# A reciprocals' row on GpSimd's queue, and two steps of the mask moved, in a masked attention kernel

## Chip, core and metric

The kernel runs on one core of one Trainium2 chip. The metric is the time of one execution in microseconds (us); the time before is the median of three runs. A profile, taken from one more execution, gives the span from the first to the last instruction and every instruction's place in it. Engines go by the profile's names: PE (TensorE), PEld (its weight load), DVE (VectorE), ACT (ScalarE), POOL (GpSimd), SP (SyncE, which here only issues DMAs). A "q" behind an engine's name is its queue of DMA issues and semaphores.

## What is computed

Eight batches of `x` (512 features by 1024 tokens, fp32) go through one attention layer with a 0/1 mask over tokens, and the result is added to `x`. Queries, keys and values are one and the same projection.

```
B, D, T = x.shape                       # 8, 512, 1024; NH = 8 heads, dk = 64
q  = transpose(x) @ Wq.T
qh = q split in heads
scores = einsum(qh, qh) / sqrt(dk)
logits = (scores * cmask + (1 - cmask) * -1e30) * rmask     # mask over keys, mask over queries
attn   = softmax(logits)
ctx    = attn @ qh
out    = x + transpose(ctx @ Wo.T)
```

A masked query has all its logits at zero, so its context is the mean over all tokens; masked keys get no weight in the other rows.

## The kernel before

Only the kept tokens are computed. For each batch the kept tokens (about half) are gathered into `NK` = 544 rows; the last row stands for the mean. All heads are taken in pairs: `pairs` holds 32 of them, numbered from 0, four to a batch (pair 11 is batch 2's last). A pair is worked through in `NC` = 5 slots, one for each chunk of 128 keys (the last is smaller). The tuple `(b, pr, c)` in `plan` names batch, pair in the batch, slot.

One slot does, in this order on all engines' queues: `scores` (TensorE, then ScalarE's exp into `e`, or `el` in slot 4), `open_slot`, the next pair's projection in slots 0 and 1, `weigh_behind` (the values weighed by earlier `e`), then the slot's tasks. Tasks come from a plan written out by hand: `put(b, pr, c, task, *args, rank=...)`. Within a slot, tasks of rank under 5 come in order of rank, then `contexts`, then those of rank 5 and over, then `issue_stores`. Every engine and every DMA queue runs its share strictly in the order in which it was written.

A gate orders TensorE against readers of its banks: `note(read)` keeps the first noted reader of a slot, and the first weighing matmul of the next slot waits for it; with none noted, it waits for the slot's own first exp:

```
gate[0] = reader[0] or reader[1]
```

What the change touches:

- `invert(pair)` runs in slot 0 of the next pair. It forms the reciprocals of the softmax sums (`ris`), turns them (`rt`), writes them in four small DMAs to a DRAM tile `row` (L788), and reads that back in two DMAs, spread over 64 partitions each, as `rb` (L793). SyncE issues all six. `contexts(pair)` multiplies by `rb`; for pair p it stands in slot 1 of pair p + 2, but for pair 27 in slot 3 of pair 28 and for pair 29 in slot 4 of pair 30. It begins with `sum_last` (L803).
- SyncE's queue also carries the pieces of `x` for batches ahead (L376), the rows stored to DRAM by `turn` (`xd`, L413), ranks (L450), output stores (L922) and `load_rows` (L902, L906), which loads tiles `g` to which results will be added.
- GpSimd's queue carries `gather` (L472, kept rows by index), stores of results to DRAM (`od`, L846) and `fetch` (L943), which adds rows of `od` to a tile `g` by index. A fetch needs its `g` loaded and its `od` stored. `finish_blocks` (VectorE, L913) then turns the tile for the store.
- Batch 0 is fetched by blocks: `place_blocks` (L891) copies the places of its tokens into `block_origin` in 16 small casts on VectorE, in slot 2 of pair 2.
- The mask is read a second time in another order (`mixed`). `rank_mixed` in pair 0, slot 3, turns it on TensorE, copies it on ScalarE (`mcol`, L1129), and ranks it by matmuls (L1133, L1134); the ranks go to DRAM and `load_ranks(1)` reads them back in slot 4. `search` (L462) uses them from pair 1, slot 2.

Of the kernel before, what the change touches and what calls it, by code (L numbers as in the profile page):

```python
# [305 lines left out]
def attention_of_kept_tokens(ctx, tc, x, mask, wq, wo, out, ident, wqT, woT, verdict, flag):  # L306


    nc = tc.nc
    B, D, T = x.shape  # L310
    P = 128
    DK = D // NH
    SCALE = 1.0 / math.sqrt(DK)
    ND = D // P
    NT = T // P
# [41 lines left out]
    seen = {}  # L357
# [3 lines left out]
    def bank(name, tag="t"):  # L361
        return ps.tile([P, NB], F32, tag=tag, name=name, bufs=2)
# [275 lines left out]
    def note(read):  # L638
        reader[0] = reader[0] or read.ins.name
# [139 lines left out]
    def invert(pair):  # L779

        b, pr = pair
        inverses(pair)
        ri = ris[pr % 2]
        rt = sb.tile([P, Q], F32, tag="rt", name=f"rt_{b}_{pr}")
        nc.vector.transpose(rt, ri)
        row = dr.tile([2, NC, A, Q], F32, tag="row", name=f"row_{b}_{pr}")
        for a in range(A):
            nc.sync.dma_start(  # L788
                row[:, :, a, :].rearrange("h c j -> (h c) j"), rt[a * Q : a * Q + 2 * NC, :]
            )  # L790
        rb = sb.tile([P, W], F32, tag="rb", name=f"rb_{b}_{pr}")
        for h in range(2):
            nc.sync.dma_start(  # L793
                rb[h * DK : (h + 1) * DK, :],
                row[h].rearrange("c a j -> (c a j)").partition_broadcast(DK),
            )
        rbs[pair] = rb
# [14 lines left out]
        nc.vector.tensor_copy(cT[:, NK - 1 : NK], qms.pop(pair))  # L812


    ods, gs, wholes, pos = {}, {}, {}, {}

    def place_outputs(b):
        if b not in ods:
# [68 lines left out]
    def place_blocks():  # L887

        for a in range(A):
            for j in range(A):  # L890
                nc.vector.tensor_copy(  # L891
                    block_origin[a * Q : (a + 1) * Q, j::A],
                    placed[j * Q : (j + 1) * Q, 0, a * (NT // A) : (a + 1) * (NT // A)],
                )
# [71 lines left out]
    def issue_stores(n=1):  # L966
        for store in stores[1]:
            store()
        stores[1] = stores[0][:n]
        stores[0] = stores[0][n:]  # L970

    pairs = [(b, pr) for b in range(B) for pr in range(ND)]
# [146 lines left out]
        for a in range(A):  # L1119
            nc.sync.dma_start(mixed[mids, a * Q : (a + 1) * Q], by_blocks[a])  # L1120

    def rank_mixed():


        BC = B * NT
        mixed, totals, spread, mcol = (seen[k] for k in ("mixed", "totals", "spread", "mcol"))
        pt = bank("mixed_t")
        nc.tensor.transpose(pt[:, :BC], mixed, ident[:BC, :BC])
        nc.scalar.copy(mcol, pt[:, :BC])  # L1129
        nc.vector.tensor_reduce(totals[:, 0:1], mixed, axis=AX.X, op=ALU.add)  # L1130
        nc.vector.tensor_copy(spread[:, 0, :], totals[:, 0:1].to_broadcast([BC, P]))
        pr = bank("rank_mixed_t")
        nc.tensor.matmul(pr[:BC, :P], mcol, seen["upto"], start=True, stop=False)  # L1133
        nc.tensor.matmul(  # L1134
            pr[:BC, :P],
            seen["before"].rearrange("p b c -> p (b c)"),
            spread[:, 0, :],
            start=False,
            stop=True,
        )  # L1140
        rank = seen["rank"] = keep.tile([BC, P], F32, tag="mixed_rank", name="mixed_rank")
        note(nc.scalar.copy(rank, pr[:BC, :P]))
        nc.sync.dma_start(ranks, rank)
# [35 lines left out]
    def plan():  # L1179
# [5 lines left out]
        def put(b, pr, c, task, *args, rank=0):  # L1185
            todo[b, pr, c].append((rank, task, args))
# [16 lines left out]
        for n in range(1, B):  # L1203
# [7 lines left out]
            else:  # L1211
                b = n - 2
# [69 lines left out]
            put(last, 3, 1 + i, begin_output, last, i, rank=7)  # L1282
        for d in range(ND):
            put(0, 3, 3 + d // 2, turn_outputs, d, rank=7)
        put(0, 0, 3, rank_mixed, rank=7)
        put(0, 0, 4, load_ranks, 1)
        put(0, 1, 1, place_all, rank=1)
        put(0, 1, 3, turn_places, rank=7)
        for b in range(2, B):
# [4 lines left out]
    def late(n):  # L1294
# [29 lines left out]
        for p, pair in enumerate(pairs):  # L1324
            b, pr = pair
            before = pairs[p - 1] if p else None
            final = p + 1 == len(pairs)
            for c in range(NC):
                scores(pair, c)
                open_slot()  # L1330
                if c == 0 and not final:
                    project(pairs[p + 1], 0)
                weigh_behind(pair, before, c)
                if c == 0 and before:
                    end_values(before)
                    if final:
                        inv = inverses(before)
                    else:
                        invert(before)
                tasks = sorted(todo[b, pr, c], key=lambda t: t[0])  # L1340
                for rank, task, args in tasks:
                    if rank < 5:
                        task(*args)
                if final and c == 0:
                    spread(before, inv)
                elif final and c == 1:
                    contexts(before)
                for earlier in settled[p, c]:
                    contexts(earlier)
                for rank, task, args in tasks:  # L1350
                    if rank >= 5:
                        task(*args)
                issue_stores(1 + (b == B - 1))
        last = pairs[-1]
        open_slot()
        weigh_behind(None, last, 0)
# [121 lines left out]
```

## Time and profile before

| | us |
|---|---|
| median of three runs | 677.13 (675.56 to 678.43) |
| the profiled execution's own time | 679.92 |
| its span | 677.9 |
| PE busy in the span | 621.4 (92%) |
| DVE busy | 362.0 (53%) |
| ACT busy | 360.5 (53%) |
| POOL busy | 184.1 (27%) |

The mean granted clock of TensorE was 0.963 of full speed. A busy share is an average over stages: the start (to about 41 us), 32 pairs of some 18 us, and the last batch's end (from about 645 us). Rows of a timeline give start, duration, engine, line, operation, and in brackets the idle time before and what ended it; a "x4" at the end means that four instructions were merged. Rows of the chain of waits give start, duration and what lay on the chain. A row of busy time by stage gives the stretch, its length, then the busy time of each engine with the number of its instructions.

### The profile page before, as it was taken

The page shows a single profiled execution, that of the slowest core. Times are in us where ns is not written, and L with a number is a line of the kernel's source. Part 1 is how long each engine was busy: PE and PEld are TensorE (multiplying, and loading weights), DVE is VectorE, ACT ScalarE, POOL GpSimd, SP SyncE. Part 2 cuts the span into 40 slices and gives each one's busy share as a digit, 9 for nine tenths or more (in the row PEclk, how much of TensorE's full clock was granted, in tenths as well). Part 3 has the DMA queues.
Part 4 walks back from the last instruction along what each step waited for, and adds up shares of the span by engine and source line. Part 5 has one row for each costly group of instructions (what it writes and reads, how often), then busy time and mean ns, then how long its engine had stood idle before and what let it go on. Part 6 is the DMA issues. An engine that isn't in the chain of part 4 may idle for free.

```text
span 677.9 us, 21834 instructions
## 1 busy us (share of the span) xinstructions
PE 621.4 (92%) x9056; PEld 413.2 (61%) x9056; DVE 362.0 (53%) x1113; ACT 360.5 (53%) x1010; POOL 184.1 (27%) x203
## 2 busy tenths in 40 slices
PE   6578989999999979999999999999999999998953
PEld 5345657677666656667666666676666655554422
DVE  6325885654564555555664566457645535234252
ACT  5127667656655645556656665656655445544300
POOL 4600221100134212341224304331334207006240
PEclk9688999999999989999999999999999999998985
DMA  8533663533366865696769777785857468744666
GB/s 277 170 122 98 197 192 89 165 97 113 103 197 141 215 185 154 205 252 164 198 227 247 169 187 247 195 196 150 233 135 144 130 212 154 211 146 78 128 197 190
DMA packets 98544, 117.10 MB, mean 173 GB/s; under 512 B 11785, under 2 KB 65625, under 8 KB 98426
## 3 DMA queue, kind: packets, MB, share of 16 engines
q1 hardware_dynamic: 77976, 75.71, 37.4%
q0 software_dynamic: 16224, 37.71, 24.4%
q10 hardware_dynamic: 4226, 2.10, 1.1%
q8 instruction: 75, 1.23, 0.8%
q14 instruction: 43, 0.35, 0.2%
HBM read 72.81 MB, written 42.67 MB: 170 GB/s over the span
## 4 chain that ended last, share of the span: by engine, by line
PE 76%; DMA 8%; DVE 7%; ACT 3%; SPq 2%; issue 2%; POOL 1%; DVEq 0%; ACTq 0%; POOLq 0%
PE s L662 17%; PE av L709 17%; PE pq L542 15%; PE po L834 15%; PE v L579 3%; DMA x<-in_x_dram 2%; PE pa L861 2%; PE xc L485 2%; DVE len L601 1%; ACT e L685 1%; DVE xc L488 1%; PE top L615 1%; PE s L676 1%; DMA rb<-row 1%; DMA g<-od,origin 1%
## 5 line engine op out<-in xcount | busy, mean ns | idle before, releaser
L685 ACT ACTIVATE e<-s,bias 128x544 f32<-128x544 f32 x256 | 180.3, 709 | 89.1 <-PE s L662 88.7
L709 PE MATMUL av<-e,v 64*64 64x272 f32 x2048 | 162.5, 398 | 7.9 <-ACT el L685 4.3
L662 PE MATMUL s<-qT 64*64 64x272 f32 x2048 | 155.8, 399 | 0.0
L542 PE MATMUL pq<-xc,wqT 64*64 64x272 f32 (+1 forms) x1984 | 127.5, 390 | 0.2 <-DVE xc L488 0.2
L709 PEld LDWEIGHTS av<-e,v 64*64 64x64 f32 x2048 | 85.5, 134 | 52.6 <-ACT cT L738 8.5
L834 PE MATMUL po<-woT,cT 128*128 128x256 f32 (+2 forms) x624 | 114.7, 363 | 0.0
L662 PEld LDWEIGHTS s<-qT 64*64 64x64 f32 x2048 | 82.3, 134 | 36.2 <-issue 6.9
L542 PEld LDWEIGHTS pq<-xc,wqT 64*64 64x64 f32 x1984 | 79.2, 134 | 37.5 <-issue 0.8
L943 POOL DMA_INDIRECT g<-od,origin x48 | 75.8, 1578 | 84.8 <-DMA g<-xd 60.5
L834 PEld LDWEIGHTS po<-woT,cT 128*128 128x128 f32 (+1 forms) x624 | 79.2, 164 | 28.8 <-issue 15.1
L846 POOL DMA_DIRECT2D od<-oc x56 | 31.3, 562 | 202.6 <-ACT oc L841 200.4
L472 POOL DMA_INDIRECT xin<-xd,source x40 | 39.8, 995 | 130.8 <-DMA row<-rt 71.8
L488 DVE COPY xc<-xc 128x512 f32<-128x512 f32 (+1 forms) x37 | 22.0, 613 | 61.4 <-PE xc L485 61.4
L559 DVE COPY qT<-pq 128x272 f32<-128x272 f32 x32 | 14.1, 439 | 70.2 <-PE pq L542 65.2
L841 ACT COPY oc<-po 128x256 f32<-128x256 f32 (+2 forms) x57 | 21.7, 382 | 55.8 <-PE po L834 55.8
L685 ACT ACTIVATION_READ_ACCUMULATOR e<-s,bias 128x1 f32 x256 | 50.2, 196 | 0.0
L588 DVE COPY v<-v 128x320 f32<-128x320 f32 x64 | 28.3, 483 | 34.3 <-PE v L579 34.3
L913 DVE STREAM_TRANSPOSE whole<-g 128x512 f32<-128x512 f32 x56 | 37.4, 687 | 13.8 <-DMA g<-od,origin 9.1
L601 DVE TENSOR_REDUCE len<-sq 128x10 f32<-128x640 f32 x32 | 26.1, 814 | 30.5 <-ACT sq L595 30.4
L738 ACT COPY cT<-av 128x272 f32<-128x272 f32 x62 | 21.1, 389 | 37.6 <-PE av L709 37.5
L425 ACT ACTIVATE junka<-x 128x512 f32<-128x512 f32 x64 | 40.2, 628 | 0.7
L462 DVE TENSOR_SCALAR_CACHE_REDUCE junk<-rank,key 128x1024 f32<-128x1024 f32 (+4 forms) x40 | 39.8, 996 | 0.0
(156 smaller groups left out, 633.4 us busy)
## 6 DMA issues: line engine op xcount, KB each, us to landing
xd<-xt SPq DMA_DIRECT2D x120, 128.0 KB
x<-in_x_dram SPq DMA_DIRECT2D x56, 256.0 KB
g<-xd SPq DMA_DIRECT2D x48, 256.0 KB
out_dram<-whole SPq DMA_DIRECT2D x20, 512.0 KB
rb<-row SPq DMA_DIRECT2D x60, 160.0 KB
od<-oc POOLq DMA_DIRECT2D x28, 256.0 KB
out_dram<-whole SPq DMA_DIRECT2D x16, 256.0 KB
rank<-ranks SPq DMA_DIRECT2D x7, 512.0 KB
```

The lines of the kernel that those rows point to most:

```text
L425: nc.scalar.activation(junk, xs[b][r][:, d, :], AF.Copy, accum_out=xbars[b][:, d, r : r + 1])
L462: nc.vector.tensor_scalar(junk[:, :n], rank[:, i * P :], key[:, col], 0.0, ALU.is_le, ALU.add, accum_out=found[:, col])
L472: nc.gpsimd.indirect_dma_start(out=xin[:n, :], out_offset=None, in_=rows_of_x[b], in_offset=bass.IndirectOffsetOnAxis(ap=searches[b][2][:n ...
L542: mm = nc.tensor.matmul(pqs[pair][hf][heads[h], :n], wqT[rows, d, at : at + DK], xcs[b][rows, d, hf * KH : hf * KH + n], start=(not cross ...
L601: nc.vector.tensor_reduce(lengths, sq.rearrange("p c (h d) -> p (c h) d", h=2), axis=AX.X, op=ALU.add,)
L662: nc.tensor.matmul(s[h][to, hf, :KH], qT[heads[h], at : at + DK], qT[heads[h], hf * KH : (hf + 1) * KH], start=True, stop=True,)
L685: act = nc.scalar.activation(e[:, h], of[h], AF.Exp, bias=biases[pair][:, c : c + 1], scale=SCALE, accum_out=acc[:, h, c : c + 1],)
L709: mm = nc.tensor.matmul(avs[pair][hf][heads[h], :KH], v[rows, c, heads[h]], e[rows, h, hf, :] if c < LAST else e[rows, h, :], start=(c == ...
L834: nc.tensor.matmul(po[j * n : (j + 1) * n, cols], cTs[b, pr][:, i * P : i * P + n], woT[:, pr, j * w + cols.start : j * w + cols.stop], st ...
L846: nc.gpsimd.dma_start(od[places[i], j * w : (j + 1) * w], oc[j * n : (j + 1) * n, :w])
L913: nc.vector.transpose(whole.rearrange("p (d a) n -> p a d n", a=A)[:, :, :, i * Q : (i + 1) * Q], gs.pop((b, i)).rearrange("p (a d f) -> p ...
L943: nc.gpsimd.indirect_dma_start(out=gs[b, i], out_offset=None, in_=ods[b], in_offset=bass.IndirectOffsetOnAxis(ap=origin[:, b, i : i + 1] i ...
```

## The change

Three things are moved.

1. The four stores of `row` are issued by GpSimd instead of SyncE. The two loads of `rb` leave `invert` for a function of their own, `load_inverses`, which runs at the end of slot 1 instead of in slot 0, behind that slot's `issue_stores`. For pair 27 (run in pair 28, the first of the last batch) it runs at the end of slot 0.
2. The 16 casts of `place_blocks` are made by GpSimd instead of VectorE.
3. `rank_mixed` is cut in two: `turn_mixed` (turning, copying, totals) stays in pair 0, slot 3; the ranking goes to slot 4 with rank 3, and `load_ranks(1)` to pair 1, slot 0.

```
 def invert(pair):
...
         for a in range(A):
-            nc.sync.dma_start(
+            nc.gpsimd.dma_start(
                 row[:, :, a, :].rearrange("h c j -> (h c) j"), rt[a * Q : a * Q + 2 * NC, :]
             )
+        inverted[pair] = row
+
+    def load_inverses(pair):
+
+        b, pr = pair
+        row = inverted.pop(pair)
         rb = sb.tile([P, W], F32, tag="rb", name=f"rb_{b}_{pr}")
         for h in range(2):
             nc.sync.dma_start(
...
 def place_blocks():
         for a in range(A):
             for j in range(A):
-                nc.vector.tensor_copy(
+                nc.gpsimd.tensor_copy(
                     block_origin[a * Q : (a + 1) * Q, j::A],
...
-    def rank_mixed():
-
+    def turn_mixed():
...
         nc.scalar.copy(mcol, pt[:, :BC])
         nc.vector.tensor_reduce(totals[:, 0:1], mixed, axis=AX.X, op=ALU.add)
         nc.vector.tensor_copy(spread[:, 0, :], totals[:, 0:1].to_broadcast([BC, P]))
+
+    def rank_mixed():
+
+        BC = B * NT
         pr = bank("rank_mixed_t")
-        nc.tensor.matmul(pr[:BC, :P], mcol, seen["upto"], start=True, stop=False)
+        nc.tensor.matmul(pr[:BC, :P], seen["mcol"], seen["upto"], start=True, stop=False)
...
-        put(0, 0, 3, rank_mixed, rank=7)
-        put(0, 0, 4, load_ranks, 1)
+        put(0, 0, 3, turn_mixed, rank=7)
+        put(0, 0, 4, rank_mixed, rank=3)
+        put(0, 1, 0, load_ranks, 1)
...
                 issue_stores(1 + (b == B - 1))
+                if before in inverted and (c == 1 or p == len(pairs) - ND):
+                    load_inverses(before)
```

More of the change, by code (lines that the diff above doesn't have):

```diff
@@ L812, in contexts @@
         nc.vector.tensor_copy(cT[:, NK - 1 : NK], qms.pop(pair))
-    ods, gs, wholes, pos = {}, {}, {}, {}
+    ods, gs, wholes, pos, inverted = {}, {}, {}, {}, {}
     def place_outputs(b):
@@ L1136, in rank_mixed @@
             seen["before"].rearrange("p b c -> p (b c)"),
-            spread[:, 0, :],
+            seen["spread"][:, 0, :],
             start=False,
```

## The prediction, made before the result was known

> **What bounds the kernel now.** I read the page first (its busy times, the first line), then busy time by stage (the other four: stretch, its length, busy time of TensorE, its weight load, VectorE, ScalarE and GpSimd with their instructions, TensorE's granted clock, the DMA engines' share, GB/s), then the order of time on each engine around the stages where TensorE is not full.
>
> ```profile
> PE 621.4 (92%) x9056; PEld 413.2 (61%) x9056; DVE 362.0 (53%) x1113; ACT 360.5 (53%) x1010; POOL 184.1 (27%) x203
> 41.50:61.40 19.90, 16.42 (x239) 10.20 (x238) 6.26 (x16) 11.96 (x36) 0.00 (x0) 0.85 0.12 31
> 76.30:95.00 18.70, 15.84 (x267) 10.12 (x263) 15.08 (x52) 11.33 (x32) 7.80 (x11) 1.00 0.77 234
> 236.00:262.20 26.20, 22.17 (x311) 14.62 (x313) 13.41 (x42) 12.49 (x37) 2.49 (x3) 0.87 0.69 189
> 262.20:334.74 72.54, 72.17 (x1124) 49.71 (x1127) 43.27 (x132) 43.86 (x125) 22.10 (x22) 1.00 0.74 201
> ```
>
> In the stretch from 262.20, one whole batch, TensorE is busy 72.17 of 72.54 us at full clock: no shorter queue can win anything there. The other three rows are the stages that this change can touch, and each holds one long wait of TensorE. The timeline of TensorE names them (in brackets the idle time before, and what ended it):
>
> ```profile
> 57.46 0.43 PE L1133 MATMUL rank_mixed_t<-upto,mcol 128*64 128x128 f32 x2 [2.58 <-ACT mcol L1129]
> 89.21 1.15 PE L709 MATMUL av<-e,v 64*64 64x272 f32 x16 [1.81 <-DVE v L588]
> 250.51 1.35 PE L579 MATMUL v<-ident,qT 64*64 64x64 f32 x40 [4.03 <-DVE qm L565]
> ```
>
> The three parts of the change each meet one of them: the ranking split the first, the block places the second, the reciprocals' row the third.
>
> **The row and its load (the third wait).** VectorE stood in `finish_blocks(0, 7)`, in front of `qm`, until the last fetch of batch 0 had landed; that fetch stood on GpSimd until its tile was loaded; and SyncE issued that load (L906) late, behind two pairs' rows:
>
> ```profile
> 241.62 0.67 DVE L913 STREAM_TRANSPOSE whole<-g 128x512 f32<-128x512 f32 x1
> 246.94 0.71 DVE L913 STREAM_TRANSPOSE whole<-g 128x512 f32<-128x512 f32 x1 [4.66 <-DMA g<-od,block_origin]
> 225.79 1.59 POOL L943 DMA_INDIRECT g<-od,block_origin  x1 [6.06 <-DMA x<-in_x_dram]
> 241.89 1.53 POOL L943 DMA_INDIRECT g<-od,block_origin  x1 [9.96 <-DMA row<-rt]
> 201.81 1.41 SPq L788 DMA_DIRECT2D row<-rt  x4
> 205.21 1.09 SPq L793 DMA_DIRECT2D rb<-row  x2
> 225.94 1.87 SPq L788 DMA_DIRECT2D row<-rt  x4
> 230.86 1.09 SPq L793 DMA_DIRECT2D rb<-row  x2
> 234.15 1.89 SPq L906 DMA_DIRECT2D g<-xd  x4
> ```
>
> The releaser of the 241.89 row is one semaphore's name; the tile's load fits in time (issued until 236.04, 5.85 us before), the row does not. Ahead of that load the change takes from SyncE the pair-10 slot-0 block, the row's four stores and their landing (225.94 to 230.86, 4.92 us) with the 1.09 us load behind it, and from the pair before the stores and their landing (201.81 to 205.21, 3.40 us; that pair's `rb` load stays ahead). Together 9.4 us. On GpSimd four row stores come in front of the last four fetches of the batch:
>
> ```profile
> L846 POOL DMA_DIRECT2D od<-oc x56: 496/539/1218, 146.6 to 613.7; - x56
> ```
>
> I price each by this row, the nearest direct DMA of that queue: 0.54 us, so 2.2 us per pair, from 2.0 to 4.9. The last fetch then goes at 241.89 - 9.4 = 232.5 by its load, or by its queue at 225.79 + 2.2 + three fetches of 1.59 = 232.8 and the gaps between them, say 233.7. It lands 5.05 us later as now (241.89 to 246.94), at 238.8, while VectorE comes for it at 241.62 + 0.67 = 242.3. The margin is 3.5 us, so the wait goes whole. VectorE then needs the 3.6 us that it needs now (246.94 to 250.51), to 245.9; TensorE is busy until 250.51 - 4.03 = 246.5, so it is itself what is late next. The worth is read from whole pairs:
>
> ```profile
> 237.46 1.15 PE L662 MATMUL s<-qT 64*64 64x272 f32 x16
> 262.19 1.08 PE s L662 x16
> ```
>
> From the pair's first scores to the next pair's (a row of the timeline, and one of the chain of waits) it takes 24.7 us; a quarter of the next batch's 72.54 is 18.1. I take 6.5 of the difference: the 4.03 us wait, and the slow clock behind it (0.87 in the stage's row). If the transfers rather than the queue set the landing, as little as nothing of it comes.
>
> Elsewhere the moves cost nothing while their cover holds. In the first slot of a batch the four stores come ahead of `gather`, which goes 2.2 us later, and what it brings is used 28 us on; in a batch's third pair they come ahead of fetches that VectorE takes a pair later:
>
> ```profile
> 186.15 1.01 POOL L472 DMA_INDIRECT xin<-xd,source  x1 [0.35 <-PE pq L542]
> 214.05 0.60 PE L485 MATMUL xc<-ident,xin 128*128 128x128 f32 x4
> ```
>
> `rb` is used a pair after its row, so a slot later is free, but for pair 27 (its `contexts` stands three slots on, so its load stays in slot 0; the last two rows are of the chain of waits):
>
> ```profile
> 557.18 0.54 POOL L846 DMA_DIRECT2D od<-oc  x1 [4.94 <-ACT oc L841]
> 560.40 1.66 POOL L943 DMA_INDIRECT g<-od,origin  x1 [2.67 <-DMA od<-oc]
> 566.83 0.20 DVE L803 TENSOR_TENSOR rb<-rb 128x64 f32<-128x64 f32 x1
> 244.43 3.16 DMA rb<-row
> 82.12 4.65 DMA rb<-row
> ```
>
> GpSimd is free at 557.72 and waits anyway until 560.40, so the stores (to about 560.2) fit. Landed 2.7 us later, as `od` was, the row lets SyncE load `rb` at 562.9, and it lands in 3.16 to 4.65 us, at 566.1 to 567.6, against 566.83. Late by 0 to 0.8, and the loss is no more; if each issue takes 1.22, 2.7 more. I take 0.3. SyncE now waits for the row at the end of slot 1; queued behind it are the `x` pieces, `load_rows` and `xd` stores of slot 2 on, and of those the fetches wait first, two or three slots later. Since SyncE reaches that place with the row's stores behind it on another queue, I cost it at nothing; the last rival takes it up.
>
> **Block places (the second wait).**
>
> ```profile
> 85.36 0.84 PE L579 MATMUL v<-ident,qT 64*64 64x64 f32 x35
> 86.21 1.19 PE L662 MATMUL s<-qT 64*64 64x272 f32 x14
> 84.33 3.18 DVE L891 CAST block_origin<-placed 32x2 int32<-32x2 f32 x16
> 87.54 1.25 DVE L401 STREAM_TRANSPOSE xt<-x 128x1024 f32<-128x1024 f32 x1
> 88.70 0.85 DVE L588 COPY v<-v 128x320 f32<-128x320 f32 x2
> ```
>
> Sixteen casts hold VectorE 3.18 us just ahead of the copy of `v` on which TensorE's gate waits. Without them the transpose ends at 85.6, `v` can be copied from 86.2, its first half is out at 86.7, and the scores before the gate run to 87.40. All of 1.81 us comes back; the clock was 1.00 there, so no more. On GpSimd the trace shows no such cast; even at 1 us each, 16 us are covered: the block fetches, its users, come over 100 us later (225.79 is one of them).
>
> **The ranking in two slots (the first wait).** Here I see the wait moved, not removed.
>
> ```profile
> 57.22 0.19 ACT L1129 COPY mcol<-mixed_t 128x64 f32<-128x64 f32 x1
> 59.53 0.49 ACT L685 ACTIVATE el<-s,bias 128x272 f32<-128x272 f32 x1 [0.72 <-PE s L676]
> 110.52 1.15 PE L709 MATMUL av<-e,v 64*64 64x272 f32 x16 [0.83 <-ACT el L685]
> 58.00:59.00 1.00, 1.00 (x13) 0.68 (x16) 0.15 (x1) 0.26 (x1) 0.00 (x0) 0.50 0.00 0
> ```
>
> `rank_mixed` noted its last copy as the gate of the next slot. `turn_mixed` notes nothing, so the gate falls to that slot's own first exp, as in other slots of batch 0 (the row at 110.52). ScalarE is in order and reaches that exp only behind `mcol`, at 57.41, and ends it 0.49 later, at 57.9. TensorE, free from 57.46 - 2.58 = 54.9, needs about 0.7 for the slot's eight scores (an estimate from fourteen in 1.19, quoted above) and waits 2.3 us. The weighing then begins some 0.8 us sooner than now, when rank and scores stand before it, but the rank's matmuls stand behind it, at 0.43 for the first two about as much. After the old wait the clock was 0.50 (the last row); if it falls again the two cancel, if it stays up about 1.2 us are won. I take nothing, from -1.2 to +0.3, with 0.4 for the clock staying up.
> [...]
>
> The rank load leaves its place ahead of four `xd` stores:
>
> ```profile
> 60.68 0.35 SPq L450 DMA_DIRECT2D rank<-ranks  x1
> 61.12 2.70 SPq L413 DMA_DIRECT2D xd<-xt  x4
> 69.98 1.26 DVE L462 TENSOR_SCALAR_CACHE_REDUCE junk<-rank,key 128x1024 f32<-128x1024 f32 x1
> 233.62 6.84 DMA rank<-ranks
> ```
>
> It goes 4 to 5 us later, near 65, and is wanted at 69.98. At the 6.84 us of the chain's row, in busier transfers, it would be 1.9 late, and VectorE's copy of `v` and TensorE's gate behind it as much. I take 0.5, from 0 to 1.9.
>
> **The sum.** -6.5 (row) -1.8 (places) +0 (split) +0.5 (rank load) +0.3 (pair 27) = -7.5 us. The profiled execution took 679.92 us (span 677.9), 0.4% above the median of the three runs and above the slowest, 678.43; so 672.4 for it, and 677.13 - 7.5 = **669.6** for the median.
>
> **Rivals.** *Transfers set the landing.* The stage's DMA share is 0.69 and SyncE's issues stretch; then the loads go earlier but land hardly so, pair 11 keeps most of its wait, and only the second wait is won: with a fifth of the 6.5 about 675. Against it: 9.4 us are freed and 4.66 are needed.
> *GpSimd's issues stretch.* At 1.22 us each, pair 27 loses 3.0 instead of 0.3, giving 672.3; below 673.7 it still counts as faster. For it, the longest of the 56 issues; against it, their median. [...]
> *Slower: SyncE held at the later load.* If GpSimd, in order, keeps the row behind a fetch that itself waits for SyncE, the load of `rb` blocks the next tiles, and each of the four batches 1 to 4 gets a stall like pair 11's, which stays too: 4 x 6.5 - 1.8 + 0.8 = +25, about 702. It decides once the row lands more than 3.5 us (the margin above) later than SyncE passes it now. Against it: the four stores add 2.2, and in the pairs that I read GpSimd had issued the earlier fetches by the time that the row was ready.
>
> **How the numbers follow.** Forecast 0.70, transfers 0.15, stretched issues 0.08, slower 0.07. About 0.5%, 3.4 us, is what a measurement here can tell from no change: the bounds are 673.7 and 680.5. Faster: 0.68 of the forecast, 0.05 of the second and 0.06 of the third, 0.79; same 0.14; slower 0.07. The range: low, 669.6 less the split's 1.2, the rank load's 0.5 and the runs' own 1.6 and 1.3 for what may shrink beside it, 665; high, the first rival with none of the 6.5, 669.6 + 6.5 = 676.
>
> **What would show it.** Right: no wait above 2 us of TensorE between 225 and 255; the last block fetch issued over 5 us before VectorE comes; pair 11 at about 18.2 us; the copy of `v` in pair 2 straight behind its matmuls; a wait on `el` of about 2.3 us in pair 0, slot 4, where the wait on `mcol` was. Wrong: `finish_blocks` still waiting in pair 11, row stores over 1 us each, `rb` last to arrive at L803 in pair 28, or SyncE idle at L793 longer than before.

## Result, and the profile after

| kernel | median, us | runs | lowest to highest |
|---|---|---|---|
| before | 677.27 | 12 | 675.56 to 680.17 |
| after | 674.95 | 12 | 672.92 to 678.28 |

The ratio is 0.9964 (95% interval 0.9947 to 0.9982): 2.3 us or 0.4% faster, where 7.5 us were forecast. The direction held and the time lies within the range; two thirds of the gain are missing.

The profiled execution after took 678.28 us, span 676.5, against 679.92 and 677.9 before. Busy time, from the page, and busy time by stage (pair 0, pair 1, pair 2, pair 11, and last the stretch in which nothing was left to win before; columns as in the prediction's rows):

```profile
PE 622.5 (92%) x9056; PEld 411.6 (61%) x9056; DVE 359.4 (53%) x1097; ACT 360.3 (53%) x1010; POOL 248.7 (37%) x339
40.68:60.75 20.07, 16.72 (x239) 9.59 (x238) 6.26 (x16) 12.42 (x37) 0.00 (x0) 0.84 0.11 28
60.75:77.04 16.29, 15.54 (x259) 9.54 (x259) 12.20 (x39) 10.07 (x29) 3.46 (x6) 0.91 0.81 240
77.04:94.64 17.60, 16.55 (x278) 10.95 (x270) 12.98 (x40) 11.71 (x33) 11.43 (x30) 1.00 0.59 184
236.21:254.41 18.20, 18.20 (x298) 12.42 (x297) 12.53 (x38) 11.57 (x34) 2.90 (x6) 1.00 0.67 176
262.20:334.74 72.54, 69.04 (x1020) 46.95 (x1016) 39.43 (x120) 40.05 (x115) 27.33 (x32) 0.95 0.71 186
```

Pair 11 is full: 18.20 us, TensorE busy throughout, clock 1.00. But the last row, in which TensorE was busy for 72.17 of 72.54 us at full clock, now has 3.5 us without work and a clock of 0.95 (the same stretch of time; it now runs from the middle of pair 12 to the start of pair 16). The timelines of TensorE, GpSimd and VectorE name what is gone, what moved and what is new:

```profile
57.09 2.09 PE L709 MATMUL av<-e,v 64*64 64x272 f32 x16 [2.45 <-ACT el L685]
88.00 1.10 PE L709 MATMUL av<-e,v 64*64 64x272 f32 x14
245.05 0.75 PE L579 MATMUL v<-ident,qT 64*64 64x64 f32 x40
227.91 1.54 POOL L949 DMA_INDIRECT g<-od,block_origin  x1 [0.31 <-issue]
240.36 1.26 DVE L919 STREAM_TRANSPOSE whole<-g 128x512 f32<-128x512 f32 x2
292.86 1.68 PE L485 MATMUL xc<-ident,xin 128*128 128x128 f32 x8 [3.16 <-DVE m L617]
291.91 0.71 DVE L919 STREAM_TRANSPOSE whole<-g 128x512 f32<-128x512 f32 x1 [4.32 <-DMA g<-od,origin]
282.99 1.66 POOL L949 DMA_INDIRECT g<-od,origin  x1 [7.44 <-DMA rb<-row]
566.55 1.15 PE L709 MATMUL av<-e,v 64*64 64x272 f32 x16 [0.73 <-DVE v L588]
```

The first row is the moved wait, at 2.45 us. The next four show the second and third wait gone: no bracket in front of the weighing at 88.00 or of `v` at 245.05; the last block fetch goes at 227.91, and VectorE takes the tiles at 240.36 without a wait. The three rows at 282 to 293 are a like stall a batch later: the first fetch of batch 1 goes late (the name in its bracket isn't what held it, see below), VectorE stands 4.32 us for it, and TensorE 3.16 us behind VectorE. The last row is pair 28.

Where the time went, pair by pair (from one pair's first scores, L662, to the next pair's, in the two profiled executions):

| | before | after | difference |
|---|---|---|---|
| pair 1 (split) | 14.82 | 16.29 | +1.5 |
| pair 2 (block places) | 19.62 | 17.59 | -2.0 |
| pair 11 (row) | 24.66 | 18.20 | -6.5 |
| pairs 13 and 14 (new stall and slow clock behind it) | 36.98 | 43.27 | +6.3 |
| pair 28 | 18.03 | 19.03 | +1.0 |
| start, pair 0, pair 16, tail | | | -1.6 |
| span | 677.9 | 676.5 | -1.4 |

The two big gains came as forecast, and most of them was given back in places that the forecast had priced at 0 to 0.5 us.

### The profile page after: what moved, and what is told of

Read it like the earlier page. It is cut to its first block, busy times and chain, and to the rows that moved or that the text cites. A ratio compares the mean times of both kernels' runs of the same rounds, so it can differ in the third digit from the quotient of the medians.

```text
span 676.5 us, 21843 instructions
## 1 busy us (share of the span) xinstructions
PE 622.5 (92%) x9056; PEld 411.6 (61%) x9056; DVE 359.4 (53%) x1097; ACT 360.3 (53%) x1010; POOL 248.7 (37%) x339
## 4 chain that ended last, share of the span: by engine, by line
PE 76%; DVE 7%; DMA 6%; issue 4%; ACT 3%; POOL 2%; SPq 1%; DVEq 0%; POOLq 0%; ACTq 0%
PE s L662 17%; PE av L709 16%; PE pq L542 16%; PE po L840 14%; DMA g<-od,origin 3%; PE v L579 2%; PE xc L485 2%; PE pa L867 2%; DVE len L601 2%; DVE xc L488 1%; PE top L615 1%; ACT e L685 1%; PE s L676 1%; DMA x<-in_x_dram 1%; DMA row<-rt 1%
## 5 line engine op out<-in xcount | busy, mean ns | idle before, releaser
L662 PE MATMUL s<-qT 64*64 64x272 f32 x2048 | 156.9, 400 | 0.0
L542 PE MATMUL pq<-xc,wqT 64*64 64x272 f32 (+1 forms) x1984 | 129.4, 395 | 0.2 <-DVE xc L488 0.2
L709 PEld LDWEIGHTS av<-e,v 64*64 64x64 f32 x2048 | 84.1, 133 | 54.0 <-ACT el L685 9.4
L662 PEld LDWEIGHTS s<-qT 64*64 64x64 f32 x2048 | 82.4, 134 | 36.8 <-issue 7.6
L788 POOL DMA_DIRECT2D row<-rt x120 | 61.6, 522 | 70.2 <-DVE rt L785 63.1
L472 POOL DMA_INDIRECT xin<-xd,source x40 | 38.4, 959 | 53.9 <-PE av L709 12.2
```

The costliest lines, as they stand in the source:

```text
L472: nc.gpsimd.indirect_dma_start(out=xin[:n, :], out_offset=None, in_=rows_of_x[b], in_offset=bass.IndirectOffsetOnAxis(ap=searches[b][2][:n ...
L542: mm = nc.tensor.matmul(pqs[pair][hf][heads[h], :n], wqT[rows, d, at : at + DK], xcs[b][rows, d, hf * KH : hf * KH + n], start=(not cross ...
L662: nc.tensor.matmul(s[h][to, hf, :KH], qT[heads[h], at : at + DK], qT[heads[h], hf * KH : (hf + 1) * KH], start=True, stop=True,)
L709: mm = nc.tensor.matmul(avs[pair][hf][heads[h], :KH], v[rows, c, heads[h]], e[rows, h, hf, :] if c < LAST else e[rows, h, :], start=(c == ...
L788: nc.gpsimd.dma_start(row[:, :, a, :].rearrange("h c j -> (h c) j"), rt[a * Q : a * Q + 2 * NC, :])
```

## Experiments

Questions: is the stall in pair 13 made by the row's part, and through what ("bunching": the row lands late, SyncE stands at the later load, its transfers bunch and the next batch's first fetch comes late), or is TensorE merely ahead of the transfers ("supply")? What does the split cost by itself? And was the gain in pair 11 as large as one execution showed ("over-read")?

The kernel before takes 677 to 679 us on some chips and 691 to 693 on others. Each ratio is taken on one chip; profiles are compared among chips of the first kind unless said. "Places" is the block places on GpSimd.

| run | edit | us | before, same chip | ratio |
|---|---|---|---|---|
| row_only | row's part alone | 677.89 | 678.45 | 0.9981 (0.9946 to 1.0016) |
| places_only | places alone | 673.10 | 678.45 | 0.9916 (0.9886 to 0.9946) |
| split_only | split alone | 683.61 | 678.45 | 1.0078 (1.0046 to 1.0110) |
| load_slot3 | all, `rb` loaded in slot 3 | 673.02 | 678.45 | 0.9909 (0.9875 to 0.9944) |
| no_split | row and places | 689.46 | 692.32 | 0.9962 (0.9928 to 0.9995) |
| no_split_slot3 | the same, `rb` loaded in slot 3 | 693.50 | 692.32 | 1.0027 (0.9995 to 1.0059) |
| row_sync | all, row's stores on SyncE | 690.76 | 692.32 | 0.9977 (0.9950 to 1.0004) |
| od_sync | all, four `od` stores on SyncE | 688.02 | 692.32 | 0.9943 (0.9921 to 0.9965) |
| whole_again | all | 676.28 | 678.69 | 0.9965 (0.9934 to 0.9996) |
| od_sync_again | as od_sync | 674.18 | 678.69 | 0.9937 (0.9912 to 0.9962) |
| no_split_slot3_again | | 674.14 | 678.69 | 0.9933 (0.9906 to 0.9960) |
| places_again | | 674.72 | 678.69 | 0.9956 (0.9938 to 0.9974) |
| row_again | | 692.86 | 693.20 | 0.9986 (0.9947 to 1.0024) |
| no_split_od_sync | no split, `od` stores on SyncE | 690.17 | 693.20 | 0.9950 (0.9915 to 0.9984) |
| no_split_od_sync_again | | 686.79 | 691.98 | 0.9926 (0.9898 to 0.9955) |

### The three parts alone

Each applies its own lines of the diff to the kernel before, and nothing else.

> The kernel before with the first part alone: the row stored by GpSimd, its load a slot later. Two theories of why the whole change won 2.3 us and not 7.5. Bunching: the fourth row store waits on GpSimd for a store of results issued eight DMAs earlier, SyncE stands at the load of rb in pair 12 until the row has landed, its loads then go out together, and the first fetch of batch 1 comes late; TensorE waits about 3 us in pair 13 with a slow clock behind it. Supply: with pair 11's wait gone TensorE is simply ahead of the transfers, and the same wait shows two pairs on. Both expect 6.5 us won in pair 11 and 2 to 6 lost in pair 13 and 14: 673 to 676 us. If the time is near 670, the loss in the whole change comes from its other parts.

> The kernel before with the second part alone: the 16 casts on GpSimd. The 1.81 us wait in pair 2 goes. If pair 11's wait has a length of its own (bunching), the time falls by 1.8 to 675.5 us. If the landing of the last block fetch stands at a time of its own (supply), TensorE comes there 1.8 sooner and waits 1.8 longer: 677.3 us.

> The kernel before with the third part alone: the second mask turned and ranked in two slots. Moved wait: a wait of 2.4 us on the exp of slot 4 where the wait on mcol was, the clock halved behind it, and the rank load later: 677.3 to 679 us. If the split does what its place in the plan suggests, 2.6 us of wait and the slow clock behind it go: 673 to 675 us. Supply: nothing won or lost before pair 11 shows, 677.3 us.

Measured: row 0.9981, places 0.9916, split 1.0078. Only the places win clearly and the split loses clearly. The row's part has pair 11 at 18.20 and gives it back in pair 13 (20.20), pair 28 (19.02) and the tail (68.33, against 64.61 before; the tail varies by itself, 63.51 and 68.03 in the two executions of the whole change). The places shorten more than pair 2 (17.59): pair 11, too, is at 20.51. The split's rows, of VectorE, TensorE, SyncE and by stage:

```profile
57.01 2.09 PE L709 MATMUL av<-e,v 64*64 64x272 f32 x16 [2.44 <-ACT el L685]
57.00:63.80 6.80, 6.79 (x53) 3.36 (x57) 2.50 (x13) 3.23 (x11) 0.00 (x0) 0.51 0.21 56
67.78 0.43 SPq L450 DMA_DIRECT2D rank<-ranks  x1
73.52 1.28 DVE L462 TENSOR_SCALAR_CACHE_REDUCE junk<-rank,key 128x1024 f32<-128x1024 f32 x1 [3.50 <-DMA rank<-ranks]
75.44 1.15 PE L709 MATMUL av<-e,v 64*64 64x272 f32 x16 [2.50 <-DVE v L588]
```

The wait is moved, not removed (2.44 us on `el`), and two things follow: the clock is at half for 6.8 us, and the rank load, at 67.78 behind the row's transfers on SyncE, makes VectorE wait 3.50 us and TensorE 2.50. Pair 1 takes 19.00 us instead of 14.82. In the whole change the row's stores are off SyncE, the load goes at 64.07, and nothing waits for it.

The clock's price can be read by itself. Stretches at half clock after, behind the moved wait and behind pair 13's stall:

```profile
56.93:63.75 6.82, 6.66 (x49) 3.32 (x53) 2.51 (x13) 3.25 (x13) 0.14 (x1) 0.50 0.19 49
292.45:299.27 6.82, 6.41 (x52) 3.98 (x56) 6.09 (x21) 1.97 (x6) 3.39 (x6) 0.50 0.76 176
```

and before, behind the wait on `mcol` and behind pair 11's stall:

```profile
57.85:61.26 3.41, 3.41 (x28) 2.12 (x27) 0.30 (x1) 1.96 (x8) 0.00 (x0) 0.50 0.05 14
249.00:255.82 6.82, 5.31 (x73) 3.49 (x74) 3.37 (x8) 2.12 (x5) 0.00 (x0) 0.50 0.71 197
```

In these rows the clock is at half for 3.41 us or for two such stretches, 6.82. A wait of 2.58 us cost one before; the moved wait of 2.45 us costs two in both executions of the whole change, in split_only, load_slot3 and both of od_sync, and one in row_sync. The length alone doesn't decide it: the unmoved wait of 2.58 us in no_split_slot3_again and the 2.50 us above in split_only cost none. By an estimate, 3.41 us more at half speed is up to 1.7 us of work. Pair 1 is 1.5 longer in the profile after and 2.1 in whole_again, so in the second some 0.3 us isn't accounted for.

### A later load

```
-                if before in inverted and (c == 1 or p == len(pairs) - ND):
+                if before in inverted and (c == 3 or p == len(pairs) - ND):
```

> The whole change, with the load of rb at the end of slot 3 instead of slot 1 (pair 28 unchanged). Bunching: SyncE is not held in pair 12 before the loads of slots 1 to 3, they go out one by one, the wait in pair 13 goes, 669 to 671 us. Supply: pair 13 waits as in the whole change, 674 to 676 us.

Measured: 0.9909; pair 13 falls from 22.68 to 19.97 and pair 14 from 20.59 to 18.23, with pair 28 at 18.40. The load's place matters, but a stall of 1.2 us stays. The run doesn't take the bunching away, it lessens it: SyncE still stands for the row, from 261.16 to 266.59, and then issues `rb`, three `g` loads and a piece of `x` one behind the other until 270.00.

### Without the split, and the row's stores back on SyncE

no_split takes the third part out of the change; no_split_slot3 also loads `rb` in slot 3, as above:

```
-        put(0, 0, 3, turn_mixed, rank=7)
-        put(0, 0, 4, rank_mixed, rank=3)
-        put(0, 1, 0, load_ranks, 1)
+        put(0, 0, 3, rank_mixed, rank=7)
+        put(0, 0, 4, load_ranks, 1)
```

row_sync leaves the change whole but for the stores' queue (L788):

```
-            nc.gpsimd.dma_start(
+            nc.sync.dma_start(
                 row[:, :, a, :].rearrange("h c j -> (h c) j"), rt[a * Q : a * Q + 2 * NC, :]
```

> The row's and the block places' parts together, without the split. 'Moved wait' (the split adds a second window of slow clock and a later rank load, and costs by itself): pair 0 and pair 1 take 20.0 and 14.8 to 15.0 us as in the kernel before, the wait of 2.58 us on mcol is back, and the time is 669 to 672, below the whole change's 674.95 by some 3 to 5 us. 'Bunching' says besides that nothing in pairs 11 to 14 changes by it: pair 11 at 18.2, and pair 13 keeps its stall (22 to 23 us). 'Supply' (TensorE is ahead of the transfers by what it won, so any gain in one place is given back in pair 13 or 14): the time stays at 674 to 676, since what the split took would be given back later.

> Row's stores on GpSimd, block places on GpSimd, no split, and the load of the row issued at the end of slot 3 instead of 1. 'Bunching': pair 13 near 19 to 20 us, pair 11 at 18.2, pair 2 at 17.6, pair 1 at 15.0: 667 to 670, the fastest of all. 'Supply': 673 to 676.

> The whole change, but the four row stores stay on SyncE (ahead of its other slot-0 work as before); the load alone is a slot later. It tells the new queue from the later load. 'Bunching': GpSimd's ninth store in flight no longer exists in the first pair of a batch, the row lands some 2 us after VectorE made it, SyncE stands under 2 us at the load, no burst, and pair 13's stall of 1.68 + 3.16 us is gone (pair 13 under 20.5); pair 11 keeps at 18.2 to 20.5, since only the stores' issue (1.9 us a pair) comes back to SyncE; 671 to 674. 'Supply', or the later load itself as the cause: pair 13 stays at 22 to 23 us and the time at 674 to 677.

These fell on a chip of the slower kind, and the expected times are missed by its 14 us; only ratios can be read: 0.9962, 1.0027, 0.9977. Pair 13 takes 19.04, 19.05 and 20.01, and pair 12, which is 17.37 elsewhere, 19.94, 20.69 and 18.46. TensorE there waits for nothing that the profile shows (timeline of no_split, TensorE):

```profile
266.76 0.31 PE L579 MATMUL v<-ident,qT 64*64 64x64 f32 x3 [0.26 <-issue]
267.79 0.33 PE L579 MATMUL v<-ident,qT 64*64 64x64 f32 x4 [0.73 <-issue]
269.20 0.48 PE L579 MATMUL v<-ident,qT 64*64 64x64 f32 x15 [1.08 <-issue]
```

So on that chip pair 12 is longer by 1.1 to 3.3 us, and the fetch gains that time. Whether leaving out the split wins by itself isn't shown: 0.9962 stands beside 0.9964 of the whole change on another chip. row_sync does show one thing: with the later load kept and only the stores back on SyncE, the first fetch of batch 1 goes 3.31 us after pair 13's first scores, as in the kernel before (3.22 or 3.23 in its four executions); in no_split, on the same chip, it goes 6.63 us after them. SyncE's waiting at the row's load, 115.5 us in all in the whole change, is 5.2 us in row_sync, but that proves little: SyncE then stands at the stores instead, 208.9 us for VectorE's `rt` (166.3 before).

### Fewer DMAs in flight on GpSimd

In the first pair of a batch GpSimd issues five `od` stores and four row stores, and the fourth row store waits (timeline of GpSimd, after; the second row is SyncE's load of the row):

```profile
257.10 1.52 POOL L788 DMA_DIRECT2D row<-rt  x3
262.33 0.51 POOL L788 DMA_DIRECT2D row<-rt  x1 [3.71 <-DMA od<-oc]
265.74 1.09 SPq L799 DMA_DIRECT2D rb<-row  x2
```

In the trace of the kernel after, the 307 DMAs of GpSimd's queue take eight completion semaphores in turn (numbers 112 to 119). The fourth row store, the ninth DMA here, has the same one (117) as the first, an `od` store issued at 254.18 that landed at 262.05, and goes 0.28 us after that landing. od_sync takes four of the nine away:

```
-            nc.gpsimd.dma_start(od[places[i], ...], oc[...])
+            queue = nc.gpsimd if parts == 1 else nc.sync
+            queue.dma_start(od[places[i], ...], oc[...])
```

> The whole change, but the four stores of the last chunk's output (the four parts of 16 KB a batch) are issued by SyncE instead of GpSimd, so that GpSimd has one od store and four row stores in a batch's first pair instead of nine DMAs. 'Bunching' by the ninth DMA: the wait of 3.71 us ahead of the fourth row store in pair 12 is gone (and those of 2.02 and 0.83 in pairs 20 and 24), SyncE's longest wait at the row's load falls from over 10 us to 4 to 7, and pair 13 from 22.7 to 19 to 20.5: 671 to 674. If the fourth store still waits as long, it is not the number of DMAs in flight on GpSimd; if the wait is gone and pair 13 stays at 22 to 23, the row's lateness isn't what makes the stall.

> The whole change again, beside the kernels of this call. In the run of it above pair 13 stalled (22.7 us), while four kernels run beside each other later all had longer first pairs of a batch instead (18.5 to 20.8 in place of 17.4 in pair 12) and no stall in pair 13. 'Bunching': if pair 12 is at 17.4, pair 13 is at 22 to 23 and pair 14 over 20; if pair 12 is longer by 1 to 3 us, the fetch has that much more time and pair 13 is below 20.5. The ratio is 0.994 to 0.999 either way. 'Supply': the same, but a stall also in the kernels beside it wherever pair 12 is at 17.4.

> The whole change with the last chunk's four od stores issued by SyncE, beside the whole change. 'Bunching' by the ninth DMA in flight on GpSimd: no wait ahead of the fourth row store, the row's load in pair 12 issued 2 to 4 us sooner than in the whole change, and 1 to 4 us less in all (ratio to the kernel before 0.990 to 0.995). 'Supply': pair 13 as in the whole change and the same time within 1 us.

Measured side by side on one chip: the whole change 676.28 us, without the ninth DMA 674.18. The intervals of the ratios overlap. In the two profiles, pairs 13 and 14 take 20.53 and 19.92 us in whole_again (3.5 us above 18.75 and 18.23), and exactly 18.75 and 18.23 in od_sync_again. GpSimd and VectorE in od_sync_again:

```profile
256.84 2.00 POOL L788 DMA_DIRECT2D row<-rt  x4
279.42 1.66 POOL L950 DMA_INDIRECT g<-od,origin  x1 [1.81 <-issue]
289.59 0.70 DVE L920 STREAM_TRANSPOSE whole<-g 128x512 f32<-128x512 f32 x1
```

The four stores go in one piece, the fetch goes at 279.42 instead of 282.56 in whole_again (counted from pair 13's first scores, 4.6 us sooner), and VectorE doesn't wait. But the expected way is wrong in one step: SyncE's load of the row goes at 263.66, hardly sooner than the 263.90 of whole_again (7.2 against 8.8 us after pair 12's first scores). The fetch doesn't wait for the row, nor for a tile: in the profile after, the loads by SyncE that it waits for had landed by 276.57. It waits for the `od` store just ahead of it on GpSimd, which goes 0.60 us after pair 13's first scores in every execution. GpSimd in the kernel before (store and fetch) and in places_again (fetch):

```profile
280.09 0.61 POOL L846 DMA_DIRECT2D od<-oc  x1 [1.74 <-ACT oc L841]
282.71 1.63 POOL L943 DMA_INDIRECT g<-od,origin  x1 [2.01 <-DMA od<-oc]
277.56 1.63 POOL L943 DMA_INDIRECT g<-od,origin  x1 [5.06 <-DMA od<-oc]
```

In these two the fetch goes 0.27 us after that store has landed. With the row's stores on GpSimd it doesn't. Its wait for the semaphores, and the fetch itself, after and in od_sync_again (of the fetch's line; the semaphore row gives min/median/max in ns):

```profile
L949 POOLq EVENT_SEMAPHORE  x3: 17/17/3417, 275.9 to 283.3; - x3
L950 POOLq EVENT_SEMAPHORE  x5: 17/43/1745, 276.8 to 279.7; - x5
```

The wait in `after` begins at 275.92 and ends 3.42 later, at 279.34 (the `od` store issued at 272.38 has landed); yet the fetch starts at 282.99, 3.65 us on. What its bracket names, a load of `rb`, isn't the cause: no_split and row_again have the same delay with nothing landing on that semaphore until over 1.6 us after it. In od_sync_again the wait ends at 278.70, and the fetch starts 0.72 later. All eight runs with nine such DMAs (the whole change twice, row_only, row_again, load_slot3, no_split and no_split_slot3 twice) have the same 3.46 us from the end of that wait to the end of the fetch's next one; the four with five have 0.53. The profile shows nothing in between. So there is a fixed delay of 2.9 us at this one instruction, which came with the row's stores on GpSimd and went when four DMAs left the queue; its cause stays open. The casts on GpSimd aren't it, since row_only, without them, has it too. It stands at batch 1 alone: in pairs 17, 21 and 25 of the profile after, the first fetch follows its store's landing by 0.27, 0.75 and 1.10 us.

That a late fetch is what makes the stall can be read across the executions on chips of the first kind. The second column is the fetch's start less pair 13's first scores; it is the 0.60 to the `od` store's issue and the two columns behind it.

| execution | fetch after pair 13's start, us | `od` store, issue to landing | landing to fetch | pair 13, us |
|---|---|---|---|---|
| before | 3.22 | 2.36 | 0.27 | 18.75 |
| split_only | 3.23 | 2.36 | 0.27 | 18.75 |
| places_only | 3.84 | 2.97 | 0.27 | 18.75 |
| od_sync_again | 5.57 | 4.22 | 0.75 | 18.75 |
| places_again | 6.27 | 5.40 | 0.27 | 18.74 |
| load_slot3 | 8.73 | 4.45 | 3.68 | 19.97 |
| no_split_slot3_again | 9.42 | 5.14 | 3.68 | 20.16 |
| row_only | 9.91 | 5.63 | 3.68 | 20.20 |
| whole_again | 10.13 | 5.85 | 3.68 | 20.53 |
| after | 11.21 | 6.93 | 3.68 | 22.68 |

Up to 6.3 us late costs nothing, from 8.7 on each later fetch costs more. The lateness has two parts. One is the delay behind the landing, 3.4 us more than before. The other is the landing: 6.93 us after against 2.36 before. While the store was under way, SyncE's transfers moved 1.80 MB after and under 0.01 MB before; TensorE reaches pair 13 at 271.78 instead of 279.49, 7.7 us sooner, while SyncE had issued its loads ahead of it by 271.06 instead of 272.94, 1.9 us sooner. That these transfers slow the landing is argued from this, not tested.

places_again has the slow landing without the delay (5.40 us, beside 0.94 MB), and no stall. no_split and row_again, on chips of the slower kind, have the delay without the slow landing (2.35 and 2.36 us, then 3.68), so that the fetch is 6.6 us late, and pair 13 takes 19.04 and 19.02 us, as in the kernel before on such chips (19.07 to 19.12). So neither part alone cost anything in these runs; the stall came where both met. "Supply" is right for the first part and wrong as the whole cause; "bunching" at the row's later load isn't what the first part needs, since places_again has it with the load where it was. Without the fixed 2.9 us the whole change would stand at 7.2 and 8.3, between what cost nothing and what cost 1.2 us.

> Places and row on GpSimd, no split, row's load at the end of slot 3. On the chip of its first run it was 1.0027 of the kernel before, with 2 to 4 us more in each first pair of a batch (12, 16, 20, 24), where TensorE idled without a wait that the profile shows. If that is of that chip (its kernel before took 692 instead of 677), it is now at 0.985 to 0.990 with pair 12 at 17.4 and pair 13 under 20.5. If it is of the load at slot 3 without the split, pairs 12, 16 and 20 are again at 20 us or more, and the ratio over 0.997.

Measured 0.9933, pair 12 at 17.37 and pair 13 at 20.16: its 1.0027 belonged to that chip, but 0.985 to 0.990 is missed, since the fixed delay is still there.

### How much was there to win in pair 11

> The block places on GpSimd alone. The first run gave 0.9916 of the kernel before, more than the 1.81 us of its wait, since pair 11 was shorter by 4.2 us as well (its wait 2.39 us instead of 4.03, without the slow clock behind it). If that belongs to the edit (VectorE or SyncE earlier in batch 0), pair 11 is again near 20.5 and the ratio 0.990 to 0.993. If it was by chance of that execution, pair 11 is at 24 to 25 and the ratio 0.996 to 0.998, which is the 1.8 to 2.0 us of pair 2 alone.

Pair 11 is at 18.44 in places_again, and the ratio 0.9956. So with the places alone pair 11 is all but free here, and 4.1 us below the first profile in places_only, though split_only, without them, is as low (20.28). SyncE's load of the last tile (L906) goes at 227.93 instead of 234.15, and GpSimd's fetch at 236.22 instead of 241.89 (GpSimd, VectorE and TensorE of places_again):

```profile
236.22 1.53 POOL L943 DMA_INDIRECT g<-od,block_origin  x1 [10.41 <-DMA g<-xd]
241.26 0.71 DVE L913 STREAM_TRANSPOSE whole<-g 128x512 f32<-128x512 f32 x1 [0.78 <-DMA g<-od,block_origin]
244.83 0.81 PE L579 MATMUL v<-ident,qT 64*64 64x64 f32 x40 [0.32 <-DVE qm L565]
```

Of those 6.2 us, TensorE's lead (2.0 us won in pair 2) explains a third; the rest are shorter waits and issues on SyncE, argued from its timeline and not tested.

> The kernel before, once more with a profile. 'The gain was there and was given back' (bunching and split): pair 11 takes 24 to 25 us with a wait of about 4 us behind finish_blocks, as in the profile that the forecast was made from. 'The gain was over-read from one execution': pair 11 takes 19 to 22 us here, with a wait under 2.5 us, and the median of the kernel before holds less of it than 6.5 us.

> The same kernel in a further execution, for the spread of pair 11 and of the tail (pair 31 and the end, 64.6 us in the first profile): 'given back' 24 to 25 us again; 'over-read' some other value between 18.5 and 25.

> The kernel before with a profile. If it runs at 675 to 681 us, as on the chip of the first profile: 'given back' has pair 11 at 24 to 25 us with a wait near 4 us; 'over-read' at 19 to 22.5 us with a wait below 2.5 us. At over 688 us it repeats the two runs above: pair 11 between 19 and 23.

These fell on chips of the slower kind (spans 688.6, 693.5, 690.9). Pair 11 takes 19.81, 22.27 and 20.23 us, with waits of 1.69, 2.21 and 2.07; pair 2 takes 23.56, 23.19 and 25.74. TensorE's rows, one of each kernel:

```profile
255.34 0.81 PE L579 MATMUL v<-ident,qT 64*64 64x64 f32 x40 [1.69 <-DVE qm L565]
257.27 1.29 PE L579 MATMUL v<-ident,qT 64*64 64x64 f32 x40 [2.21 <-DVE qm L565]
257.84 0.81 PE L579 MATMUL v<-ident,qT 64*64 64x64 f32 x40 [2.07 <-DVE qm L565]
```

"Over-read" is borne out in part: 24.66 is the longest of the seven executions without the row's part for which it is known (18.44, 19.81, 20.23, 20.28 of split_only, 20.51, 22.27 and it). What the kernel before takes there in a second execution on a chip of the first kind wasn't seen.

> The row's part alone, again. 'Given back': pair 11 at 18.2, and pairs 13 (20 or more), 28 (19.0) and the tail (over 66) longer than in the kernel before, ratio 0.995 to 1.001. If the tail of 68.3 in its first run was that execution's own, it is 64 to 66 here and the span 673 to 675, with the ratio still above 0.990.

0.9986, pair 11 at 18.20, pair 13 at 19.02 with pair 12 at 20.31, the tail 66.17. The row's part by itself is worth 0.1 to 0.2%, within what can be told from nothing.

### Both suspected losses taken out

> The whole change without the split, and with the last chunk's four od stores issued by SyncE. 'Given back by split and ninth DMA': pair 1 at 14.8 to 15.8, pair 2 at 17.6, 11 at 18.2, 13 at 18.75, 14 at 18.23, so 7 to 8 us below the kernel before in the profile and a ratio of 0.987 to 0.991, the lowest of all. 'Over-read' or 'supply': no better than the block places alone, 0.992 to 0.996.

> The whole change without the split, with the last chunk's od stores on SyncE. On a chip at 677 us for the kernel before: pair 1 at 14.8 to 15.8, 2 at 17.6, 11 at 18.2, 13 at 18.75, 14 at 18.23, ratio 0.987 to 0.991 by 'given back'; 0.991 to 0.994 by 'over-read', since then the kernel before loses less in pair 11 than its first profile shows. On a chip at over 688: 0.992 to 0.998 again.

Measured 0.9950 and 0.9926, both on chips of the slower kind, where pair 13 takes 20.20 and 19.43. Not the lowest: places alone (0.9916, 0.9956) and the load in slot 3 (0.9909, once) are as good. od_sync is below the kernel before on both of its chips (0.9943, 0.9937), and beside the whole change it is 2.1 us below that too; the intervals don't separate those two.

## Why the prediction was right or wrong

**Block places, -1.8: right in its pair, short in all.** Pair 2 fell by 2.0 us, the weighing at 88.00 waits for nothing, and the 16 casts took 2.9 us on GpSimd, under cover. But alone the edit is worth 3.0 to 5.7 us (0.9956 and 0.9916 of some 678). The rest presumably comes in pair 11, as the two profiles of it suggest; then the working was wrong to take the two terms as independent.

**Row, -6.5: mechanism right, size probably over-read.** The last fetch went at 227.91, 12.4 us before VectorE came (over 5 forecast), pair 11 took 18.20 (18.2 forecast), and the row stores 0.52 us each (0.54 taken). The term was the difference of one execution, whose own time was above the slowest of the three timed runs; the other six executions above had 0.2 to 4.1 us to win there. And with the places made faster, pair 11 had only 0.2 and 2.3 us left to win.

**The row's stores on GpSimd, "elsewhere the moves cost nothing while their cover holds": the step that failed.** The working priced the four stores by their issue, 2.2 us a pair, and looked at what stands behind them in a batch's first and third pair and in the last batch. It didn't look at the second pair, whose first fetch stands behind them too. In pair 13 that fetch went 11.21 us after the pair's first scores instead of 3.22. Of these 8.0 us, 3.4 are the delay on GpSimd's queue, which no run without the row's stores there has, and 4.6 the slower landing of the `od` store, beside transfers of SyncE with which TensorE, 7.7 us sooner there, has caught up (argued, as said above). VectorE then stands 4.32 us and TensorE 3.16 behind it: +6.3 us in pairs 13 and 14 in the profile after and +3.5 in whole_again. Only batch 1 stalled, since only there the two met. The delay's size couldn't be read before; that a fetch stood there could.

The last rival named the consequence, a stall like pair 11's a batch on, but another way to it: SyncE held at the later load, "costed at nothing", at a chance of 0.07. SyncE's wait at that line did rise, one of the signs of being wrong, from 50.4 us in 45 waits (longest 3.8) to 115.5 in 27 (longest 15.8):

```profile
SPq L799 <- DMA row<-rt: 115.5, 27, 15.8
```

But od_sync_again keeps 82.3 us of it, longest 15.5, without a stall, and the late fetch didn't wait for a tile. With the load in slot 3 the stall was 1.2 us, so the load's place may have a share; how large wasn't separated. The ninth DMA's wait on GpSimd (6.6 us in three places) was missed too, but it doesn't reach the fetch by GpSimd's order: pair 13's `od` store goes 0.60 us after the first scores with it and without.

**Split, 0, and rank load, +0.5: the wait right, the sum too small.** 2.45 us on `el` against 2.3 forecast. The cost is +1.5 in pair 1 (2.1 in whole_again), most of it since the clock falls for two stretches instead of one (6.82 us instead of 3.41, by the estimate above up to 1.7 us of work); the case priced at -1.2 (clock stays up) didn't come. How long a wait must be for the clock to fall isn't shown: it fell behind 2.45 us here, and no slow stretch followed 2.50 us in split_only and 2.58 us in no_split_slot3_again. The rank load behind the row cost 2.5 us where the row's stores were still ahead of it, beyond the bound of 1.9, and nothing in the whole change.

**Pair 27, +0.3: +1.0 and +0.6** (in pair 28), beyond the 0.8 given for stores of normal length, and by another way. After, VectorE doesn't wait for `rb` (its load goes at 559.75, the multiplication at 566.82); it stands 2.58 us for a fetched tile at 565.41, where it stood 1.33 before, and TensorE 0.73 behind it.

**Rivals.** Transfers setting the landing: not in pair 11, which is clear; in pair 13 a landing did stretch (6.93 us against 2.36). GpSimd's issues stretching: no, the longest of 120 row stores took 602 ns.

**The sum.** With the terms as the two profiles have them, -2.0 - 6.5 + 6.3 + 1.5 + 1.0 - 1.6 = -1.3 us for the profiled execution, which is the spans' -1.4 but for rounding. The median's -2.3 is larger; the profile after is of the slowest of its 12 runs, so the usual stall is presumably below 6.3. How long it usually is wasn't shown.

## What to carry to other kernels

A stall removed from one queue can come back on the queue that gets the instructions, as here: between the two profiles TensorE's wait of 4.03 us in pair 11 went and one of 3.16 us in pair 13 came. Before moving DMAs, count what is in flight there (here the ninth waited, up to 3.71 us) and find the first consumer behind them, in every part of the cycle, here a fetch a batch on. What is won upstream also brings the consumers sooner to transfers that don't come as much sooner: here TensorE 7.7 us, SyncE's loads 1.9. A wait read from one profile is one draw (pair 11 without the row's part took 18.44 to 24.66 us); check the profiled execution's own time against the timed runs, and don't add up gains that stand behind the same queue. A TensorE wait of some 2.5 us cost its own length and none, one or two stretches of 3.41 us at half clock here, so a wait moved by a slot isn't free.

## What was not expected of the hardware

- GpSimd's ninth DMA in flight waited for the first one's landing: 3.71 us in pair 12, 2.02 in pair 20, 0.83 in pair 24.
- A fixed 3.46 us on GpSimd's queue behind a satisfied wait of one fetch, the same to 0.01 us in eight runs, and 0.53 in four with four DMAs fewer a batch; cause open.
- A landing that stretches: the same `od` store took 2.36 us from issue to landing before and 6.93 after, beside under 0.01 MB and 1.80 MB of SyncE's transfers.
- No fixed price of a wait in clock: 2.45 us of idle TensorE was followed by two stretches of 3.41 us at half clock in six executions and by one in row_sync, and 2.58 us by one before and by none in no_split_slot3_again.
- Chips differ: the kernel before takes 677 to 679 us on some and 691 to 693 on others, where TensorE also idles without a visible wait (0.26, 0.73 and 1.08 us in a row in no_split).
